# A two-layer attention and expert kernel: layer 0's sum over the experts in seven half-block products instead of eight, with two PSUM banks each for the scores and the scans

## The chip, the cores and the metric

The kernel runs on one core of a Trainium2 chip. The core has a matrix engine (TensorE, PE in the profile, with its weight loads as PEld), a vector engine (VectorE, DVE), an activation engine (ScalarE, ACT), a general engine (GpSimd, POOL) and an engine that issues DMAs (SyncE, SP). They work on an on-chip memory, SBUF, of 128 partitions; matrix products land in PSUM, which this kernel divides into 8 banks of 512 fp32 per partition. The metric is device time in microseconds. Here the median of three runs before the change is 1165.7 us (1164.95 to 1167.74). A line such as L765 is line 765 of the kernel before.

## What is computed

Tokens x (4096 x 256, fp32) go through two layers. In layer 0 every token is normalised, and two terms are added to it: a gated attention within chunks of 32 tokens, and 16 experts which all see every token, each weighted by its own sigmoid. In layer 1 there are four gated linear scans (of which the router mixes two per token) and eight larger experts, of which each token takes one. Only layer 0's experts matter to the change:

```python
def _L0_ffn_ref(input_tensor, expert_sel, keys, values):   # xn, (16, 256), (16, 256, 128), (16, 128, 256)
    sel = jax.nn.sigmoid(jnp.einsum('bsd,ed->bse', input_tensor, expert_sel))
    scores = jax.nn.relu(jnp.einsum('bsd,edh->bseh', input_tensor, keys))
    out = jnp.einsum('bseh,ehv,bse->bsv', scores, values, sel)
    return out
...
xn = _layernorm(x, axis=-1)
x = x + _L0_attn_ref(xn, ...) + _L0_ffn_ref(xn, ...)
xn = _layernorm(x, axis=-1)
x = x + _L1_attn_ref(xn, ...) + _L1_ffn_ref(xn, ...)
```

`out` is a product over the 16 x 128 pairs of expert and hidden unit: a (tokens x 2048) matrix times a (2048 x 256) matrix.

## The kernel before

**Blocks and groups.** Tokens are worked in 8 blocks of 512 (`TB`; `HB` is half, 256). Features lie on the partitions, in two halves of 128 (`DC`). The 16 experts are worked in 4 groups of 4 (`EG`), each as two pairs (`SG`).

**Seven products.** A 2 x 2 blocked matrix product can be done with 7 block products and some sums of blocks in place of 8. `seven` does that (Winograd's form): `weight_sums` prepares the sums of the weights once, `column_sums` those of the tokens per block, on GpSimd. The seven products are accumulated in three PSUM banks, `px`, `py` and `pv`; ScalarE copies `px` out between products (`u1`, `u2`, `u4`: L238, L245, L249) and VectorE adds these copies to `py` or `pv` (L239, L250, L255). The kernel uses it for the queries and gates (`yg`), for the score of each expert group (`scores`) and for layer 1's scans (`scans`). `seven` is a generator that is advanced one step at a time, so that a caller can put other work between its steps.

**The sum over the experts** is not done that way before the change: `into` (L765) takes, for each expert and each 128 tokens, the 128 x 128 scores as weights and the 128 x 256 values as the moving operand: 4 products of 256 columns per expert, 64 per block, accumulated in two PSUM banks (`acc`) together with the attention's output product. At the block's end VectorE adds the two banks to the residual (L802).

**Order.** PE, SP, ACT and DVE follow the order in which the Python code emits instructions (`manual_schedule`); each engine takes its queue in order and waits at an instruction until what it needs is there. On POOL a scheduler chose the order, other than at the start and in the tail. In `experts0` a loop over the 16 experts advances `scores` of the next group by a step, emits one expert's products, and runs what the dictionary `beside` holds for this expert: `scan_step`s of the block before, pieces of the next block's layer norm (`norm0`), pieces of the routing of the block before (`norm1`), loads. A `scan_step` advances the scans by one of four steps of `seven` and emits on VectorE up to two pieces that are due (a scan is one piece, its weighing by the router another). There are 24 scan steps per block from block 2 on, 12 in block 1 and none in block 0. At a block's start comes `attention0`, which advances `norm1` of the block before (`aside`).

**PSUM.** 8 banks: `px`, `py`, `pv` for the scans (`psc1`), `a`, `b`, `c` for scores and transposes (`ps`), two for `acc` and the attention's outputs (`pacc`). The scans swap `px` and `py` from one pair to the next (`bank_of`).

**DMA.** SP loads the next group's `keys`, `vals` and `selb` (the sigmoids, broadcast to all partitions), the scans' weights `ws`, the next x. A load waits in SP's queue until the buffer is free, and with it everything behind it.

Of the kernel before, what the change touches and what calls it, by code (L numbers as in the profile page):

```python
# [51 lines left out]
def tile_two_layers(  # L52
# [39 lines left out]
    def load_x(b, parts=1):  # L92
        xs[b] = res.tile([P, NT, D], F32, name=f"x_{b}", tag="x", bufs=5)
        rows = x[b * TB : (b + 1) * TB, :].rearrange("(n p) d -> p n d", p=P)
        for n in range(0, NT, NT // parts):
            nc.sync.dma_start(out=xs[b][:, n : n + NT // parts, :], in_=rows[:, n : n + NT // parts, :])
# [43 lines left out]
    def inverse_root(y, var):  # L140

        v = small.tile([P, NT], F32, name="v_eps")
        nc.vector.tensor_scalar(v, var, EPS, None, ALU.add)
        bits = small.tile([P, NT], I32, name="bits")
        nc.vector.tensor_scalar(bits, v.bitcast(I32), 1, None, ALU.logical_shift_right)
        nc.vector.tensor_scalar(y.bitcast(I32), bits, -1.0, float(0x5F3759DF), ALU.mult, ALU.add)
        s = small.tile([P, NT], F32, name="newton")
        for _ in range(3):
            nc.vector.scalar_tensor_tensor(s, y, -0.5, y, ALU.mult, ALU.mult)
            nc.vector.tensor_mul(s, s, v)  # L150
            nc.vector.scalar_tensor_tensor(y, s, 1.5, y, ALU.add, ALU.mult)

    def layernorm(xt, xn, mv, rstd):
# [7 lines left out]
        inverse_root(rstd, mv[:, :, 1])  # L161
        yield
        for n in range(NT):
            nc.vector.tensor_scalar(
                xn[:, n, :D], xt[:, n, :], mv[:, n, 0:1], rstd[:, n : n + 1], ALU.subtract, ALU.mult
            )

    def transposed(ps, banks, dst, src):

        for c in range(DC):  # L170
            pt = ps.tile([P, TB], F32, name="pt", tag=next(banks))
            for n in range(NT):
                nc.tensor.transpose(pt[:, n * P : (n + 1) * P], src[:, n, c * P : (c + 1) * P], ident)
            nc.scalar.copy(dst[:, c, :], pt)
            yield
# [47 lines left out]
    def seven(name, w, cols, z, bank, keep):  # L223
# [18 lines left out]
        pv = bank(f"pv_{name}")  # L242
        product(7, pv, True)
# [3 lines left out]
        product(5, px, False)  # L247
# [62 lines left out]
    banks = cycle(("px", "py", "pv"))  # L310

    def bank_of(i, name):

        return name if i % 2 or name == "pv" else {"px": "py", "py": "px"}[name]

    def plain(i, z, b, s):
        w = scan_w[i]
        for ec in range(DC):
            for q, (k, m) in enumerate(PAIRS[s]):
                p = psc1.tile([P, TB], F32, name=f"p_{i}_{ec}_{q}", tag=next(banks))  # L320
# [9 lines left out]
    def scans(b):  # L330
# [44 lines left out]
        for s in range(len(PAIRS)):  # L375
# [18 lines left out]
            else:  # L394
                it = seven(
                    f"s{i}", scan_w[i], cols1[b], z,
                    lambda n, i=i: psc1.tile([P, SG, HB], F32, name=n, tag=bank_of(i, n[:2])),
                    lambda n: su.tile([P, SG, HB], F32, name=n, tag="u", bufs=4),
# [29 lines left out]
    def room(name):  # L428

        return psc1.tile([P, 2, D], F32, name=name, tag=bank_of(steps_done // CHUNKS, "py"))  # L430
# [22 lines left out]


    HALF = (1, 2, 2, 1, 1, 2, 2, 1)
    SCANS_AT = [(0,) * E0, (0,) * len(HALF) + HALF] + [HALF + HALF] * (NB - 2)
# [3 lines left out]
    def scan_step(k=1):  # L460
        nonlocal steps_done
        for _ in range(k):
            if finished and steps_done % CHUNKS == 2 and next(finished[0], 0) == 0:
                finished.pop(0)
# [5 lines left out]
            for piece in due:  # L470
                piece()

# [12 lines left out]
    with ExitStack() as l0:  # L485
# [3 lines left out]
        pacc = l0.enter_context(tc.tile_pool(name="pacc", bufs=2, space=bass.MemoryType.PSUM))  # L489


        third = cycle(("b", "c", "a"))
        spare = repeat("c")
# [26 lines left out]
        keys, vals, ksum_d = {}, {}, []  # L520
# [20 lines left out]
        def values(i):  # L541
            g = i % (E0 // EG)
            if i in vals or i >= NB * (E0 // EG):
                return
            vals[i] = wp.tile([P, EG, D], F32, name=f"vals_{i}", tag="vals", bufs=2)
            nc.sync.dma_start(out=vals[i], in_=e_vals[:, g * EG : (g + 1) * EG])
# [20 lines left out]
        def fold():  # L567
            raw = []
            for j, w in enumerate((wq, wkk)):
                r = wk.tile([P, DC, D], F32, name=f"raw_{j}", tag="rs", bufs=3)  # L570
                pt = ps.tile([P, DC, D], F32, name=f"ptw_{j}", tag=next(third))
# [8 lines left out]
            pw = ps.tile([P, DC, D], F32, name="pw", tag=next(third))  # L580
# [27 lines left out]
        def chosen(b, xnT, bank):  # L608

            psel = ps.tile([P, P], F32, name=f"psel_{b}", tag=bank)  # L610
# [6 lines left out]
        def norm0(b, out):  # L617
# [6 lines left out]
            if b == 0:  # L624
# [3 lines left out]
                pt = [ps.tile([P, TB], F32, name=f"pt_{c}", tag=next(third)) for c in range(DC)]  # L628
# [7 lines left out]
            else:  # L636
                yield from transposed(ps, spare, xnT, xn)
# [7 lines left out]
        def sevens(name, w, cols, z):  # L645
# [3 lines left out]
                lambda n: ps.tile([P, SG, HB], F32, name=n, tag={"px": "a", "py": "c", "pv": "b"}[n[:2]]),  # L649
                lambda n: wk.tile([P, SG, HB], F32, name=n, tag=n[:2]),  # L650
            )

        def attention0(b, xnT, cols, aside):
# [6 lines left out]
            def values(n):  # L660

                if n % 2 == 0:
                    pv.append(psc1.tile([P, 2, D], F32, name=f"pv_{b}_{n}", tag=("py", "pv")[n // 2]))
# [10 lines left out]
            next(aside, None)  # L674
# [3 lines left out]
            next(aside, None)  # L678
# [13 lines left out]
            pst = ps.tile([P, NT, CHUNK], F32, name=f"pst_{b}", tag="b")  # L692
            for n in range(NT):
                for c in range(DC):
                    for q in range(0, P, CHUNK):
# [4 lines left out]
                        )  # L700
            sT = wk.tile([P, NT, P], F32, name=f"sT_{b}", tag="u1")
# [28 lines left out]
        NB_G = E0 // EG  # L730

        def experts0(b, cols, selb0, att, beside):

            rs = {}

            def scores(g):
# [10 lines left out]
                it = sevens(f"{b}_{g}", keys.pop(NB_G * b + g), cols, r)  # L747
# [15 lines left out]
            def into(n, lhsT, rhs, first, stop):  # L763

                nc.tensor.matmul(  # L765
                    acc[n // 2][:, n % 2, :], lhsT, rhs, start=first and n % 2 == 0, stop=stop, skip_group_check=True
                )

            def gated(n):
                for c in range(DC):  # L770
                    into(n, og[:, c, n * P : (n + 1) * P], wo[:, c, :], c == 0, False)

            ahead = scores(0)
            next(ahead)
            next(att)
            next(ahead)
            next(att)
            next(ahead)
            og = next(att)
            acc = [pacc.tile([P, 2, D], F32, name=f"acc_{b}_{h}", tag="acc") for h in range(NT // 2)]  # L780
            next(ahead)
            for n in range(NT):
                gated(n)
            k = 0
            for g in range(E0 // EG):
                ahead = scores(g + 1) if g + 1 < E0 // EG else iter(())
                r = rs.pop(g)
                values(NB_G * b + g + 1)
                val = vals.pop(NB_G * b + g)
                for i in range(2):  # L790
                    for q in range(SG):
                        next(ahead, None)
                        for n in range(NT):
                            into(
                                n, r[i][:, q, n * P : (n + 1) * P], val[:, SG * q + i, :], False, k == E0 - 1
                            )
                        for step in beside.get(k, ()):
                            step()
                        k += 1
            for h in range(NT // 2):  # L800
                at = xs[b][:, 2 * h : 2 * h + 2, :]
                nc.vector.tensor_add(at, at, acc[h])  # L802

        def norm1(b):
# [7 lines left out]
            side = spare if b + 1 < NB else third  # L812
            yield from transposed(ps, side, xn1T[b], xn)
            if b * len(PAIRS) < FIRST_PLAIN:
                cols1[b] = column_sums(su, xn1T[b], f"sums1_{b}", 2)
            pg = ps.tile([P, P], F32, name=f"pg_{b}", tag=next(side))
# [7 lines left out]
            pl = ps.tile([P, NT, QC], F32, name=f"pl_{b}", tag=next(side))  # L824
# [28 lines left out]
            pct = ps.tile([P, P + 2 * NT * E1], F32, name=f"pct_{b}", tag=next(side))  # L853
# [44 lines left out]
        for b in range(NB):  # L898
# [7 lines left out]
            beside = {e: [] for e in range(E0)}  # L906
            if b + 2 < NB:
                beside[8].append(lambda b=b: load_x(b + 2))
            for e, k in enumerate(SCANS_AT[b]):
                if k:  # L910
                    beside[e].append(lambda k=k: scan_step(k))
            if b > 0:
                for e in (0, 1, 2, 3, 4, 5, 6):
                    beside[e].append(lambda: next(back))
            if b + 1 < NB:
                ahead = norm0(b + 1, xnT)

                for e in (5, 7, 8, 9, 10, 12, 13) if b else (3, 4, 5, 8, 9, 12, 13):
                    beside[e].append(lambda: next(ahead))
            if b == 0:  # L920
                kept = scan_sums()
                for e in (1, 2, 3, 4, 5, 6, 7, 8, 14):
                    beside[e].append(lambda: next(kept))
            if b == 1:
                beside[0].append(lambda: scan_weights(0))
            if 1 < b < NB - 1:

                for s in ((3, 4), (5,), (0,), (1,), (2,))[b - 2]:
                    beside[5].append(lambda s=s: raw_weights(s))
# [6 lines left out]
        l0_ps, between = ps, repeat("a")  # L936

        def room(name):
            return l0_ps.tile([P, 2, D], F32, name=name, tag=next(between))

        third = cycle("bc")
        back = norm1(NB - 1)
        for _ in range(3):
            next(back)
        scan_step(4)
        next(back)
        next(back)
        next(back)
        scan_step(2)
        next(back)  # L950
        scan_step(1)
        next(back)
        scan_step(1)
        next(back)
        scan_step(4)
# [12 lines left out]
    ps = ctx.enter_context(tc.tile_pool(name="ps1", bufs=5, space=bass.MemoryType.PSUM))  # L968

# [187 lines left out]
    def first_sums7(j):  # L1157
# [40 lines left out]
        pv = psc1.tile([P, FP, P], F32, name=f"pv1_{j}", tag="pv")  # L1198
# [174 lines left out]
```

## Time and profile before

| | before |
|---|---|
| median of 3 runs | 1165.7 us (1164.95 to 1167.74) |
| the profiled execution | 1166.05 us |
| its span, first to last instruction | 1164.3 us |
| mean granted TensorE clock | 0.998 |
| start to block 0's first product | 14.8 us |
| block 0, block 1, block 2 | 69.7, 93.3, 108.9 us |
| blocks 3 to 6 | 109.4 us each |
| HBM read, written | 209.0 MB, 27.1 MB |

The blocks are taken from the start of each block's first `px_yg` product. Matmuls are pipelined: a row's mean duration (380 ns for 256 columns) overlaps that of the next one, so that the pace is read from the starts of consecutive runs, not from the durations. Every fp32 product is two records in the trace: the 512 products of L765 are 1024 records. "Idle before" is the time that the engine stood still just before the instruction, with what ended it.

### The profile page before, as it was taken

How to read it: one execution, taken by the hardware profiler on the slowest of the kernel's cores; microseconds unless marked ns; L12 is line 12 of the kernel's file. 1: busy time of each engine (PE TensorE's matmuls, PEld its weight loads, DVE VectorE, ACT ScalarE, POOL GpSimd, SP SyncE). 2: the span in 40 equal slices, each digit the busy share in tenths (PEclk: the TensorE clock that was granted, in tenths of full speed). 3: DMA queues.
4: the chain of work that ended last, by engine and by line, in shares of the span. 5: the costliest groups of instructions: out<-in, count | busy, mean ns of one | idle time of the engine just before them, and what ended most of it. 6: DMA issues, size and time to landing. Idle time of an engine off the chain costs nothing. (4 is left out here: it accounts for less than half of the span.)

```text
span 1164.3 us, 17738 instructions
## 1 busy us (share of the span) xinstructions
PE 1147.5 (99%) x6426; PEld 976.8 (84%) x6426; DVE 750.1 (64%) x1568; ACT 368.1 (32%) x719; POOL 356.5 (31%) x410
## 2 busy tenths in 40 slices
PE   8999999999999999999999999999999999999997
PEld 7887888888888888888888888888744889999996
DVE  5545736687579657866786787578699435654222
ACT  3112142344343433333342343343434211111221
POOL 6182220232014120402130222011054167774433
PEclk9999999999999999999999999999999999999999
DMA  7796464475256434634654565244247866688796
GB/s 246 233 340 242 149 216 140 156 240 186 101 185 205 155 122 171 215 136 160 213 189 136 183 204 185 102 168 155 73 148 231 304 227 216 226 296 314 264 353 240
DMA packets 90442, 233.60 MB, mean 201 GB/s; under 512 B 14076, under 2 KB 43024, under 8 KB 83440
## 3 DMA queue, kind: packets, MB, share of 16 engines
q1 hardware_dynamic: 82128, 205.00, 51.8%
q0 software_dynamic: 7792, 26.91, 6.4%
q8 instruction: 52, 0.85, 0.3%
q10 hardware_dynamic: 432, 0.52, 0.1%
q14 instruction: 38, 0.31, 0.1%
HBM read 208.98 MB, written 27.09 MB: 203 GB/s over the span
## 5 line engine op out<-in xcount | busy, mean ns | idle before, releaser
L765 PE MATMUL acc<-vals,rs 128*128 128x256 f32 x1024 | 242.2, 380 | 0.0
L765 PEld LDWEIGHTS acc<-vals,rs 128*128 128x128 f32 x1024 | 194.4, 190 | 27.0 <-issue 1.4
L1223 PE MATMUL py<-w2p,hT 128*128 128x256 f32 x576 | 133.9, 380 | 0.0
L348 POOL COPY last<-z 128x1 f32<-128x1 f32 x56 | 19.6, 352 | 340.2 <-DVE z L346 340.2
L1223 PEld LDWEIGHTS py<-w2p,hT 128*128 128x128 f32 x576 | 106.1, 191 | 12.3
L306 ACT ACTIVATE z<-z,bs 128x256 f32<-128x256 f32 (+1 forms) x156 | 87.4, 611 | 1.9 <-DVE z L255 1.9
L229 PE MATMUL px_s<-sums,ws 128*128 128x256 f32 x312 | 81.4, 383 | 0.0
L229 PE MATMUL px_s<-xn1T,ws 128*128 128x256 f32 x312 | 80.2, 380 | 0.0
L229 PE MATMUL pv_s<-sums,ws 128*128 128x256 f32 x312 | 80.1, 379 | 0.0
L1129 PE MATMUL ph<-xTp,w1p 128*128 128x128 f32 (+1 forms) x512 | 75.0, 302 | 1.5 <-ACT xTp L1113 1.5
L346 DVE TENSOR_TENSOR_SCAN z<-z,last,z 128x512 f32<-128x512 f32 x56 | 75.7, 1351 | 0.0
L1129 PEld LDWEIGHTS ph<-xTp,w1p 128*128 128x128 f32 x512 | 68.8, 192 | 5.6 <-ACT xTp L1113 2.0
L743 DVE SCALAR_TENSOR_TENSOR rs<-rs,selb 128x512 f32<-128x512 f32 x64 | 69.3, 1082 | 2.1 <-DMA selb<-sel_d 1.1
L229 PE MATMUL px<-xnT,keys 128*128 128x256 f32 x256 | 69.4, 394 | 0.1
L229 PE MATMUL px<-sums,keys 128*128 128x256 f32 x256 | 66.6, 383 | 0.0
L229 PE MATMUL pv<-sums,keys 128*128 128x256 f32 x256 | 66.6, 383 | 0.0
L229 PEld LDWEIGHTS px_s<-xn1T,ws 128*128 128x128 f32 x312 | 59.3, 190 | 8.2 <-issue 0.4
L229 PEld LDWEIGHTS pv_s<-sums,ws 128*128 128x128 f32 x312 | 59.4, 190 | 8.0
L229 PEld LDWEIGHTS px_s<-sums,ws 128*128 128x128 f32 x312 | 57.3, 190 | 9.8 <-ACT u_s L245 3.2
L322 PE MATMUL p<-xn1T,wr 128*128 128x512 f32 x144 | 63.4, 595 | 1.1 <-ACT z L325 1.1
L306 ACT ACTIVATE z<-px_s,bs 128x256 f32<-128x256 f32 x78 | 32.7, 470 | 99.1 <-PE px_s L229 99.1
L1133 ACT ACTIVATE hT<-ph,b1p 128x128 f32<-128x128 f32 (+1 forms) x68 | 27.1, 398 | 112.4 <-PE ph L1129 66.8
(264 smaller groups left out, 2017.6 us busy)
## 6 DMA issues: line engine op xcount, KB each, us to landing
ws<-wsum_d SPq DMA_DIRECT2D x39, 896.0 KB, 4.9
selb<-sel_d SPq DMA_DIRECT2D x64, 512.0 KB, 6.5
w1p<-in_w_dram SPq DMA_DIRECT2D x27, 1024.0 KB, 7.1
w2p<-in_w_dram SPq DMA_DIRECT2D x27, 1024.0 KB, 9.1
keys<-ksum_d SPq DMA_DIRECT2D x28, 896.0 KB, 10.5
vals<-in_e_vals_dram SPq DMA_DIRECT2D x32, 512.0 KB, 4.6
cb<-comb_d SPq DMA_DIRECT2D x32, 256.0 KB, 10.1
wsum_d<-wst POOLq DMA_DIRECT2D x6, 896.0 KB, 7.7
```

The source lines that it names most:

```text
L229: nc.tensor.matmul(to[:, q, :], w[:, q, at, :], cols[k - 1], start=start and q == 0, stop=True, skip_group_check=True,)
L306: nc.scalar.activation(z[ec][:, q, lo:hi], src[:, q, :], AF.Tanh if i == 1 else AF.Sigmoid, bias=bs[:, i, m, ec : ec + 1])
L322: nc.tensor.matmul(p, w[:, q, 2 * ec + c, :], xn1T[b][:, c, :], start=(c == 0), stop=(c == DC - 1))
L346: nc.vector.tensor_tensor_scan(h, a[ec][:, m % 2, :], h, 0.0 if b == 0 else state, ALU.mult, ALU.add)
L348: nc.gpsimd.tensor_copy(state, h[:, TB - 1 : TB])
L743: nc.vector.scalar_tensor_tensor(r[i][:, :, lo:hi], src, 0.0, selb[i][:, :, lo:hi], ALU.max, ALU.mult)
L765: nc.tensor.matmul(acc[n // 2][:, n % 2, :], lhsT, rhs, start=first and n % 2 == 0, stop=stop, skip_group_check=True)
L1129: nc.tensor.matmul(ph, w1s[:, c, f * P : (f + 1) * P], xTp(j)[:, c, : sn * P], start=(c == 0), stop=(c == DC - 1))
L1133: nc.scalar.activation(h[:, f, :], ph, AF.Relu, bias=b1s[:, f : f + 1])
L1223: nc.tensor.matmul(py, hT[j][:, f, n * P : (n + 1) * P], w2s[:, f, :], start=(f == 0), stop=(f == FC - 1))
```

## The change

**The sum over the experts in seven products.** The scores of a group are a 2 x 2 block matrix (two halves of the block's tokens, the two experts of a pair), and so are the values (two experts, two halves of 128 output columns). `unit` emits one of seven products, for one pair, as two matmuls of 128 tokens x 128 columns. Each of the seven is accumulated by itself over the whole block in its own quarter- or half-bank (`sums`, in four `acc` banks instead of two), with 2, 3 and 4 on top of the attention's output. At the block's end one ScalarE copy and four 128 x 256 VectorE additions combine them, and three 128 x 512 additions put them on the residual; one further such addition goes earlier, into the last group.

**The sums that it needs.** `score_sums` makes four sums of scores per group, each 128 x 512, on VectorE in block 0 and on GpSimd from block 1 on. Their buffer (tag "proj") is single and shared with `yg`. `value_sums` makes four 128 x 256 sums of the values on VectorE for the four groups of block 0; SP then writes the seven blocks to DRAM (`vsum_d`), from where the later blocks load them: 896 KB per group in place of 512.

**Banks.** Scores and scans have two banks each: `pv` takes the bank of `py` once VectorE's first addition has read it. Products 5 and 7 now stand together in the third step, 7 after 5 (before it at a block's first group, `close`). Transposes, the router's products and the scans' outputs share these banks at fixed places; the next x has four buffers instead of five.

**Order.** In place of the loop over experts there is a written order per group: `u` one unit, `X` a step of the next group's scores, `s` a scan step, the rest places at which pieces stand. `ALONE` is for groups without scans beside them. Layer norm and routing are cut into more pieces; one piece of `norm1` stays in the attention, after `pst`.

```diff
-        xs[b] = res.tile([P, NT, D], F32, name=f"x_{b}", tag="x", bufs=5)
+        xs[b] = res.tile([P, NT, D], F32, name=f"x_{b}", tag="x", bufs=4)
...
-        for _ in range(3):
+        for k in range(3):
+            if k:
+                yield
...
         product(6, px, False)
-        pv = bank(f"pv_{name}")
-        product(7, pv, True)
         u2 = keep(f"u2_{name}")
         nc.scalar.copy(u2, px)
         yield
-        product(5, px, False)
+        pv = bank(f"pv_{name}")
+        for k in (7, 5) if close else (5, 7):
+            product(k, px if k == 5 else pv, k == 7)
...
-        pacc = l0.enter_context(tc.tile_pool(name="pacc", bufs=2, space=bass.MemoryType.PSUM))
+        pacc = l0.enter_context(tc.tile_pool(name="pacc", bufs=4, space=bass.MemoryType.PSUM))
...
-            vals[i] = wp.tile([P, EG, D], F32, name=f"vals_{i}", tag="vals", bufs=2)
-            nc.sync.dma_start(out=vals[i], in_=e_vals[:, g * EG : (g + 1) * EG])
+            vals[i] = v = wp.tile([P, SG, SEVEN, P], F32, name=f"vals_{i}", tag="vals", bufs=2)
+            if i < NB_G:
+                group = e_vals[:, g * EG : (g + 1) * EG].rearrange("p (q i) (k d) -> p q i k d", i=2, k=2)
+                for at, (k, h) in ((0, (0, 0)), (5, (0, 1)), (1, (1, 0)), (2, (1, 1))):
+                    nc.sync.dma_start(out=v[:, :, at, :], in_=group[:, :, k, h])
+                vsum_d.append(dram.tile([P, SG, SEVEN, P], F32, name=f"vsum_d_{g}"))
+            else:
+                nc.sync.dma_start(out=v, in_=vsum_d[g])
+
+        def value_sums(i):
+            b11, b21, b22, t1, t2, t3, t4 = (vals[i][:, :, k, :] for k in range(SEVEN))
+            nc.vector.tensor_sub(t1, t3, b11)
...
-                lambda n: ps.tile([P, SG, HB], F32, name=n, tag={"px": "a", "py": "c", "pv": "b"}[n[:2]]),
+                lambda n: ps.tile([P, SG, HB], F32, name=n, tag={"px": "a", "py": "b", "pv": "b"}[n[:2]]),
...
+        ORDER = [
+            "y0 u s y1 u s p0 y2 u y3 u X x1 u s b0 u X x2 u s b1 u u X x3 u s u s p1 u u X x4 u".split(),
+            "u s q0 u u X x1 u s b0 u X x2 u s b1 u s p0 u u X x3 u s u u X x4 u s u".split(),
+        ]
+        ALONE = [
+            "y0 u y1 u y2 u y3 u X x1 u b0 u X x2 u b1 u u X x3 p1 u u X x4 u u u".split(),
+            "q0 u u u X x1 u b0 u X x2 u b1 u u p0 u X x3 u u X x4 u u u".split(),
+        ]
+        PARTS = (1, 2, 4, 5, 7, 6, 3)
...
+            def score_sums(g):
+                a11, a12, a21, a22 = (r[:, :, h * HB : (h + 1) * HB] for h in range(2) for r in rs[g])
+                t = wk.tile([P, 4, SG, HB], F32, name=f"rsum_{b}_{g}", tag="proj")
+                eng = nc.gpsimd if b else nc.vector
+                eng.tensor_add(t[:, 0], a21, a22)
+                eng.tensor_sub(t[:, 1], a11, a21)
+                eng.tensor_sub(t[:, 2], t[:, 0], a11)
+                eng.tensor_sub(t[:, 3], a12, t[:, 2])
...
+            def unit(g, k, q, part, val):
+                for h in range(2):
+                    nc.tensor.matmul(
+                        sums[k][:, h], part[k][:, q, h * P : (h + 1) * P], val[:, q, VAL[k], :],
...
-                    for q in range(SG):
                         next(ahead, None)
-                        for n in range(NT):
-                            into(
-                                n, r[i][:, q, n * P : (n + 1) * P], val[:, SG * q + i, :], False, k == E0 - 1
-                            )
...
-            for h in range(NT // 2):
-                at = xs[b][:, 2 * h : 2 * h + 2, :]
-                nc.vector.tensor_add(at, at, acc[h])
+                if b == 0:
+                    nc.sync.dma_start(out=vsum_d[g], in_=val)
+            c1, c2 = (wk.tile([P, 2, D], F32, name=f"c_{b}_{k}", tag=k) for k in ("u2", "u4"))
+            both16 = wk.tile([P, 2, P], F32, name=f"both16_{b}", tag="u1")
+            nc.scalar.copy(c1[:, :, :P], sums[1])
+            nc.vector.tensor_add(both16, sums[6], c1[:, :, :P])
+            nc.vector.tensor_add(c1[:, :, P:], sums[5], both16)
+            nc.vector.tensor_add(c2[:, :, :P], sums[7], both16)
+            nc.vector.tensor_add(c2[:, :, P:], sums[5], c2[:, :, :P])
+            nc.vector.tensor_add(xb[:, :2, :], xb[:, :2, :], acc[0])
+            nc.vector.tensor_add(xb[:, :2, :], xb[:, :2, :], c1)
+            nc.vector.tensor_add(xb[:, 2:, :], xb[:, 2:, :], c2)
...
-        for _ in range(3):
+        for _ in range(7):
             next(back)
-        scan_step(4)
+        scan_step(5)
```

## The prediction

> **What bounds the kernel now.** I read the busy times first, then the costliest groups, then the starts of consecutive runs on PE (to get a pace, since durations overlap), and last the table of stretches and VectorE's and GpSimd's order of time.
>
> ```profile
> PE 1147.5 (99%) x6426; PEld 976.8 (84%) x6426; DVE 750.1 (64%) x1568; ACT 368.1 (32%) x719; POOL 356.5 (31%) x410
> L765 PE MATMUL acc<-vals,rs 128*128 128x256 f32 x1024 | 242.2, 380 | 0.0
> ```
>
> PE is the bound: 99% of 1164.3 us. A product taken away from it is worth its pace, as long as nothing new makes PE wait. The pace is in PE's order of time (start, duration, line):
>
> ```profile
> 502.12 1.89 PE L765 MATMUL acc<-vals,rs 128*128 128x256 f32 x8
> 503.85 0.38 PE L229 MATMUL px_s<-xn1T,ws 128*128 128x256 f32 x1
> ...
> 1091.62 3.73 PE L1129 MATMUL ph<-xTp,w1p 128*128 128x128 f32 x32
> 1095.19 0.38 PE L1111 MATMUL px<-ident,xrp 128*128 128x128 f32 x2
> ```
>
> Eight records of 256 columns take 503.85 - 502.12 = 1.73 us, 0.216 each. Thirty-two of 128 columns take 1095.19 - 1091.62 = 3.57 us, 0.1115 each. Half the columns cost almost exactly half the time, so half-sized products lose only 0.1115 - 0.108 = 0.0035 us per record.
>
> The stretches of block 0 (first row, no scans beside it) and of block 4 (second) show what VectorE has left; columns are busy us of PE, PEld, DVE, ACT, POOL, granted clock, DMA share, GB/s:
>
> ```profile
> 33.50:84.00 50.50, 50.50 (x252) 44.19 (x251) 23.25 (x47) 6.71 (x12) 25.19 (x33) 1.00 0.86 284
> 505.50:615.00 109.50, 109.50 (x613) 94.47 (x612) 81.21 (x169) 41.58 (x83) 21.79 (x26) 1.00 0.51 172
> ```
>
> VectorE is busy 74% of a block, GpSimd 20%, and the clock is full.
>
> **The change part by part.**
>
> *Products.* Before: 1024 x 0.216 = 221.2 us. After: 8 blocks x 4 groups x 7 units x 2 pairs x 2 matmuls x 2 records = 1792 records, x 0.1115 = 199.8. That is **-21.4 us**. The pace would have to reach 221.2 / 1792 = 0.123 to give it all back. Bounds: -21.4 at the pace of L1129; at the 190 ns that one weight load of L765 lasts, were loads not hidden, it would be a loss of 119, but L1129 has the same loads and runs at 0.1115, so I leave that end out.
>
> *Block 0's sums on VectorE.* Each group gets four value sums (128x256) and four score sums (128x512). Nearest rows:
>
> ```profile
> L1163 DVE TENSOR_TENSOR tsum<-xTp 128x128 f32<-128x128 f32 x8 | 2.3, 281 | 0.0
> L356 DVE TENSOR_TENSOR acc<-acc,z 128x512 f32<-128x512 f32 x48 | 38.2, 796 | 1.6
> ```
>
> 281 ns for 128 columns and 690 to 796 for 512 put 256 columns near 0.42 to 0.53; with 0.7 to 0.9 for the score sums a group costs 4.9 to 6.9 us, four groups 20 to 28. VectorE has 50.5 - 23.2 = 27 us free there, so it comes close to being full, and the scores of the next group queue behind the sums. Laying this out group by group I find PE waiting between 1 and 5.2 us for the whole block; the middle is **+3**. The six extra DMA issues on SP (0.43 to 0.6 us each, 3 us) delay `selb`: 20.48 + 7.1 = 27.6 becomes 30.6, and the first use is at 32.4, so nothing. The writes of `vsum_d` wait in SP's queue for the value sums of their own group, long done when SP, which has issued the next group's loads ahead of them, comes to them: nothing; uncovered, each would hold the loads behind it by one issue (0.6).
>
> *GpSimd's score sums, blocks 1 to 7.* 28 groups x 4 sums, of 1.27 (L1152) to 1.53 us (L341) each: 142 to 171 us on an engine that is 20% busy. Time on GpSimd is free; what it does to VectorE is not. Four rows bear on this:
>
> ```profile
> L1152 POOL TENSOR_TENSOR wsum<-w1p 128x512 f32<-128x512 f32 x8 | 10.3, 1286 | 0.1
> L1164 DVE TENSOR_TENSOR tsum<-xTp,tsum 128x128 f32<-128x128 f32 x8 | 10.1, 1262 | 0.3
> ```
> ```profile
> 598.68 1.21 DVE L355 TENSOR_TENSOR z<-z,cb 128x512 f32<-128x512 f32 x1
> 599.93 1.10 DVE L356 TENSOR_TENSOR acc<-acc,z 128x512 f32<-128x512 f32 x1
> ```
>
> L1164 runs while GpSimd is in its sums of L1152 to L1155 and takes 1262 ns; L1163, the same size, takes 281: one VectorE addition lost 0.98 us, about a whole GpSimd sum, and the four additions L1163 to L1166 together no more than 1.0. Between 596.3 and 600.4, with four smaller GpSimd sums running, L355 and L356 lose 0.5 each over their usual 0.7: 1.1 per set. So four sets add 4.0 to 4.4 us of VectorE to a block. The trace has no case with GpSimd sums in every group; bounds are nothing and L1164's full wait behind each of the four, 4 x 0.98 = 3.9 us per set. I take 1.1, since both places where it can be seen gave that.
>
> The Trainium skill, "SBUF — State Buffer", section "Who interferes with whom", speaks against this part: VectorE instructions with two operands in SBUF and GpSimd instructions that read SBUF exclude each other, the later one blocked for the other's whole length. The 1262 ns agree with it, the 1.1 us of a whole set do not reach its worst case: an estimate from that rule, with four sums of 1.29 us each blocking an addition, is 5.1 us per set, and with it the whole change would come out as a loss of some 50 us.
>
> What reaches PE is less, as VectorE runs beside PE. PE needs it in time at two kinds of place: product 7, which now overwrites the bank that L239 must have read, and the transposes, which need `xn`. Between the `py` product and product 7 of the same bank stand at least 5.2 us; L239 follows its product by 0.83 us in the median, 3.1 at most: 2.1 us of cover against a set's 1.1. Laying a steady block out by hand, PE waits 0.8 us without contention (0.5 and 0.3 at transposes in groups 0 and 2) and 3.3 with 1.1 us added in each set (1.5, 0.5, 1.3). Block 4 already has some 2.6 us of small gaps per 100 us, which these partly replace, so I take 1.5 per block, for the six blocks with full scans (2 to 7): **+9**. Bounds: 0, and 4 x (3.9 - 2.1) x 6 = 43.
>
> *The block's end.* VectorE does four 128x256 and three 128x512 additions, 4 x 0.43 + 3 x 0.7 = 3.8 us, against 1.28 in L802's pair, ahead of `yg`'s L239. `yg` issues 6.05 us of products before product 7 needs L239 done, and it is done at about 5.65: covered by 0.4 us; uncovered up to 2.5 per block. At layer 0's end the longer chain stands ahead of the last norm, with five scan steps to cover it, not four: **+0.5** (0 to 2.5).
>
> *Two banks, loads, GpSimd's order.* The swap of `pv` into `py`'s bank is priced in the cover above. `vals` grows by 0.39 MB in 28 groups, 11 MB, plus 3.7 MB written, at a DMA share of 0.51: nothing; were they not hidden, 384 KB more at block 4's 172 GB/s are 2.3 us per group. The x load goes from two blocks ahead to one, in the first group; the first layer norm on it stands in the second group, over 25 us later, and a load lands in under 11 (the longest of the page's rows): nothing. GpSimd's own queue is passed too: the router's four scatter issues (L884, 1.18 us each) stand ahead of the third group's score sums, and end about when the sums' buffer comes free; uncovered, all 4.7 us come late, against a first use some 9 us after the group begins: nothing. The column sums (0.73, 0.87, 1.40 us) stand ahead of the fourth group's score sums; those give their first result about 7 us after the group begins, and the fourth product needs it at 9: nothing, or a group's start late by up to 1.
>
> Sum: -21.4 + 3 + 9 + 0.5 = -8.9. From the profiled execution's 1166.05 that is 1157.15; the median of the runs is 0.35 below that execution, so **1157**.
>
> **The rivals.** With x for the third term, the change is x - 17.9. A measurement of this kernel can tell about 0.3%, 3.5 us, from no change.
>
> *Waits stay small* (18%): gaps only replace those there are, x = 0 and block 0 at +1: -20, 1146 (1143 to 1150). For it: 2.1 us of cover. Against: the hand layout finds transposes late.
>
> *The gain is given back* (18%): x between 14.4 and 21.4, or 2.4 to 3.6 us per block, near the 3.3 of the layout: 1167 (1162 to 1169).
>
> *Slower* (20%): in each group, VectorE's additions after L239 alternate with GpSimd's four sums, each waiting for one. A set then costs up to 3.9, L239 gets later than its cover, product 7 waits in the shared bank, and the scores behind it are late for the next sums. At 6 us per block x is 36: 1184. It decides from 3.6 us per block on. For it: L1164 shows the full wait; 81.2 + 2.6 + 4 x 3.9 = 99.4 us of VectorE in a block of 106.7 (109.4 less a block's 2.7). Against: no set in this trace lost more than 1.1.
>
> *The forecast* (44%): 1157, own range 1150 to 1162.
>
> **How the numbers follow.** Faster is forecast and small waits, 0.62; same 0.18; slower 0.20. The range takes in the forecast, the given-back case, most of small waits and the lower edge of slower: 1144 to 1173.
>
> **What would show it.** Starts of eight unit records 0.89 us apart confirm the first term. Steady blocks of some 108.2 us (109.4 - 2.7 + 1.5), with L356 and L743 longer in the mean and GpSimd busy near 500 us, confirm the third; blocks near 106.7 mean small waits, 110.3 and more the slower case, with PE's idle time named after the scores' L239 or GpSimd's sums. Block 0 should stay near 69.7 (- 2.7 + 3). I am wrong in kind if unit records keep 0.12 or more, or if PE waits for a load.

## The result, and the profile after

The changed kernel takes 1223.13 us in the median (1222.99 to 1228.84), the kernel before 1165.86 on the same chip: 1.0501 times as long, 95% interval 1.0468 to 1.0534. The forecast was 1157. The profiled execution has a span of 1221.2 us, 56.9 more than before:

| stretch | before | after | difference |
|---|---|---|---|
| start to block 0 | 14.8 | 14.2 | -0.6 |
| block 0 | 69.7 | 82.35 | +12.7 |
| block 1 | 93.3 | 98.3 | +5.0 |
| blocks 2 to 6, each | 108.9 to 109.4 | 115.4 to 116.5 | +33.5 in all |
| block 7's first px_yg to the end | 439.8 | 446.2 | +6.4 |

Busy time by engine, from the page of the changed kernel:

```profile
PE 1153.2 (94%) x7194; PEld 992.1 (81%) x7194; DVE 850.1 (70%) x1648; ACT 376.9 (31%) x727; POOL 499.0 (41%) x522
```

PE is busy 94% of a longer span; it now stands still in every block. PE's order of time shows that the cheaper products are real (start, duration, line):

```profile
82.09 1.50 PE L828 MATMUL acc<-vals,rsum 128*128 128x128 f32 x12
83.43 2.02 PE L828 MATMUL acc<-vals,rs 128*128 128x128 f32 x16
```

Twelve unit records take 1.34 us, 0.1117 each: 1792 of them 200.2 us, 21.0 less than before. The waits of PE, longest in total first (total us, times, longest):

```profile
PE pt L179 <- DVE rs L246: 25.2, 13, 4.9
PE pct L925 <- DVE z L246: 6.2, 5, 1.2
PE acc L828 <- DVE vals L559: 4.3, 1, 4.3
```

L246 is VectorE's first addition after a `py` product (L239 before). The transposes of the layer norm (`pt`) and the router's products (`pct`) use the bank that it must have read. So PE waits for a bank of the shared pair, and not for GpSimd's sums: no line names them. The place is the same in each steady block; here it is in block 4, VectorE's order of time first, then PE's and GpSimd's:

```profile
500.67 1.58 DVE L357 TENSOR_TENSOR z<-z,cb 128x512 f32<-128x512 f32 x1
502.29 1.65 DVE L358 TENSOR_TENSOR acc<-acc,z 128x512 f32<-128x512 f32 x1
...
504.46 1.70 DVE L348 TENSOR_TENSOR_SCAN z<-z,last,z 128x512 f32<-128x512 f32 x1
506.08 1.16 DVE L151 SCALAR_TENSOR_TENSOR newton<-rstd 128x4 f32<-128x4 f32 x1
...
507.55 0.68 DVE L357 TENSOR_TENSOR z<-z,cb 128x512 f32<-128x512 f32 x1
508.26 0.69 DVE L358 TENSOR_TENSOR acc<-acc,z 128x512 f32<-128x512 f32 x1
508.88 0.68 DVE L343 TENSOR_TENSOR z<-z 128x512 f32<-128x512 f32 x1
509.48 0.73 DVE L169 TENSOR_SCALAR xn<-x,mv,rstd 128x256 f32<-128x256 f32 x2
510.12 0.68 DVE L246 TENSOR_TENSOR rs<-py,u 128x512 f32<-128x512 f32 x1
```
```profile
505.81 0.59 PE L236 MATMUL py<-xnT,keys 128*128 128x256 f32 x2
...
507.55 1.03 PE L236 MATMUL pv_s<-sums,ws 128*128 128x256 f32 x4
510.86 0.44 PE L179 MATMUL pt<-ident,xn 128*128 128x128 f32 x2 [2.28 <-DVE rs L246]
```
```profile
500.44 1.26 POOL L797 TENSOR_TENSOR rsum<-rs,rs 128x512 f32<-128x512 f32 x1 [0.42 <-PE acc L828]
501.67 1.72 POOL L798 TENSOR_TENSOR rsum<-rs 128x512 f32<-128x512 f32 x1
503.35 1.72 POOL L799 TENSOR_TENSOR rsum<-rsum,rs 128x512 f32<-128x512 f32 x1
505.15 2.07 POOL L800 TENSOR_TENSOR rsum<-rs,rsum 128x512 f32<-128x512 f32 x1
```

The `py` product ends near 506.2 and the transposes in its bank are due at 508.4. L246 gets its turn at 510.1, behind everything that VectorE was late with. While GpSimd is in its four sums, a Newton step on 128x4 elements takes 1.16 us (0.16 elsewhere) and the scan 1.70 (1.27 elsewhere); earlier in the same set L357 and L358 took 1.58 and 1.65 for 0.68. L246 itself, which reads one operand from PSUM, keeps its 0.68. That set cost VectorE 0.9 + 1.0 + 0.4 + 1.0 = 3.3 us. The groups of the changed kernel say the same over the whole span:

```profile
L358 DVE TENSOR_TENSOR acc<-acc,z 128x512 f32<-128x512 f32 x48 | 47.7, 994 | 1.6
L151 DVE SCALAR_TENSOR_TENSOR newton<-rstd 128x4 f32<-128x4 f32 x48 | 21.9, 457 | 0.8
```

Before, the two had means of 796 (L356) and 185 ns (L149). The Trainium skill ("SBUF — State Buffer", "Who interferes with whom") has a VectorE instruction with two operands in SBUF and a GpSimd instruction that reads SBUF shut each other out; the 1.16 us of a 0.16 us instruction beside a sum of 2.07 fit that.

### The profile page after: what moved, and what is told of

It is laid out like the page before. It is cut to its first block, busy times and chain, and to the rows that moved or that the text cites. A ratio compares the mean times of both kernels' runs of the same rounds, so it can differ in the third digit from the quotient of the medians.

```text
span 1221.2 us, 19575 instructions
## 1 busy us (share of the span) xinstructions
PE 1153.2 (94%) x7194; PEld 992.1 (81%) x7194; DVE 850.1 (70%) x1648; ACT 376.9 (31%) x727; POOL 499.0 (41%) x522
## 5 line engine op out<-in xcount | busy, mean ns | idle before, releaser
L828 PEld LDWEIGHTS acc<-vals,rsum 128*128 128x128 f32 x1024 | 139.5, 195 | 8.4 <-issue 1.4
L828 PE MATMUL acc<-vals,rsum 128*128 128x128 f32 x1024 | 143.8, 279 | 0.0
L828 PE MATMUL acc<-vals,rs 128*128 128x128 f32 x768 | 112.2, 282 | 5.0 <-DVE vals L559 4.3
L828 PEld LDWEIGHTS acc<-vals,rs 128*128 128x128 f32 x768 | 106.4, 198 | 11.7 <-DVE vals L559 5.1
L797 POOL TENSOR_TENSOR rsum<-rs,rs 128x512 f32<-128x512 f32 x28 | 35.5, 1268 | 172.7 <-PE acc L815 141.3
L348 DVE TENSOR_TENSOR_SCAN z<-z,last,z 128x512 f32<-128x512 f32 x56 | 82.3, 1470 | 0.0
L236 PE MATMUL px<-sums,keys 128*128 128x256 f32 x256 | 72.9, 410 | 0.0
L236 PEld LDWEIGHTS pv_s<-sums,ws 128*128 128x128 f32 x312 | 58.9, 190 | 12.5 <-DVE x L447 4.7
L955 POOL DMA_INDIRECT xs_d<-xn,pos_i x32 | 32.9, 1028 | 85.8 <-DVE run L953 78.5
L236 PE MATMUL px<-xnT,keys 128*128 128x256 f32 x256 | 66.7, 383 | 0.0
```

The costliest lines, as they stand in the source:

```text
L236: nc.tensor.matmul(to[:, q, :], w[:, q, at, :], cols[k - 1], start=start and q == 0, stop=True, skip_group_check=True,)
L348: nc.vector.tensor_tensor_scan(h, a[ec][:, m % 2, :], h, 0.0 if b == 0 else state, ALU.mult, ALU.add)
L797: eng.tensor_add(t[:, 0], a21, a22)
L828: nc.tensor.matmul(sums[k][:, h], part[k][:, q, h * P : (h + 1) * P], val[:, q, VAL[k], :], start=(k in (1, 5) and g == 0 and q == 0 and h ...
L955: to = nc.gpsimd.indirect_dma_start(out=xs_d, out_offset=bass.IndirectOffsetOnAxis(ap=pos_i[:, n : n + 1], axis=0), in_=xn[:, n, :], in_of ...
```

## The experiments

Six of the kernels leave work out, so that tokens go to other experts in layer 1; they are read by their blocks. From layer 1's first expert product to the last, e1 and e3 take 262 us where the kernels with the whole computation take 255. The kernel before took 1168.2 us beside e1 to e4, 1165.0 beside e5 to e8, 1165.1 beside e9 to c1 and 1165.2 beside c2.

**e1, no sums of scores.**
```diff
-                eng.tensor_add(t[:, 0], a21, a22)      # and the other three sums
...
-                return {... 5: t[:, 0], 7: t[:, 1], 6: t[:, 2], 3: t[:, 3]}
+                return {... 5: raw, 7: raw, 6: raw, 3: raw}      # raw = xnT[b][:, :, :HB]
```


> Left out: score_sums; the units of products 5, 7, 6 and 3 read xnT, which is always ready, in place of the four sums. Nothing else is changed: banks, order and the sums of the values stay. Theory (contention: GpSimd's four sums per group lengthen VectorE's additions, VectorE comes late to the additions that free a PSUM bank and to xn, PE waits at the transposes): steady blocks fall from 116.4 to about 108 us, block 1 from 98 to 93, block 0 from 82 to 74; about 1160 us in all. Rival 1 (two banks and the new order make PE wait with or without the sums): steady blocks stay above 113 us, 1200 us or more in all. Rival 2 (PE waits for the sums themselves, as GpSimd delivers them late): as the theory here, 1160; the next kernel parts them.

Steady blocks 108.1, block 1 88.7, block 0 81.2; 1176.8 us. The sums cost a steady block 8.0 us (blocks 3 to 6: 7.3 to 8.4). Banks and order don't (rival 1 falls). Block 0 doesn't follow the theory.

**e2, the sums on VectorE in all blocks.**
```diff
-                eng = nc.gpsimd if b else nc.vector
+                eng = nc.vector
```


> score_sums on VectorE in all blocks, not only in block 0. Theory: VectorE itself takes 4 x 0.68 = 2.7 us per group for them, 11 us per block, against the 8 us that a steady block lost to contention; so PE's waits stay of the same size, steady blocks 113 to 118 us, 1205 to 1235 in all, but VectorE's other instructions go back to their usual durations. Rival 1 (banks and order): within 5 us of 1223. Rival 2 (GpSimd delivers late): the sums come 3 us after the group begins, not 7, and steady blocks fall below 110 us, 1185 or less in all.

Steady blocks 115.5 to 117.1, 1221.9 us, as the theory had it (the total fits rival 1 as well, which e1 has ruled out). L357 is back at 721 ns and L151 at 166 in the mean, and yet nothing is gained: four sums in a row on VectorE are worth as much as GpSimd's interference.

**e3, no sums at all.** As e1, and in block 0:
```diff
-                if b == 0:
-                    value_sums(g)
```


> Left out: score_sums as in the run before, and value_sums: in block 0 SP loads raw blocks of the values in all seven places (three DMA issues more per group). Theory: block 0 falls to 68 us (69.7 less 2.7 for the products, and a little for the longer block end), as the sums' VectorE time beside GpSimd's sums of weights was what made it 82; about 1152 in all. Rival 1: block 0 stays above 75 and the total above 1195.

Steady blocks 108.1 again, but block 0 takes 86.4, more than with the sums: VectorE's sums alone are not what makes it long. Total 1181.5. The steady block has this share of each engine (columns as before), and the changed kernel's block 5 that:

```profile
512.83:620.93 108.10, 107.40 (x708) 94.93 (x707) 82.45 (x176) 42.51 (x83) 18.62 (x26) 1.00 0.53 188
```
```profile
542.22:658.71 116.49, 109.92 (x709) 95.82 (x708) 90.71 (x176) 42.87 (x83) 41.35 (x42) 0.99 0.50 174
```

With equally many VectorE instructions (176), GpSimd's sums add 8.3 us to VectorE's busy time (90.71 - 82.45), 2.1 us per set, and the block is 8.4 us longer.

**e4, eight products in the new order.** The 16 old products of a group (expert and 128 tokens) are spread over the 14 `u`; two banks each, no sums, the short block end.
```diff
-                        k, q = next(units)
-                        unit(g, k, q, part, val)
+                        for i, q, n in next(slots):
+                            nc.tensor.matmul(acc[n // 2][:, n % 2, :], r[i][:, q, n * P : (n + 1) * P], val[:, SG * q + i, :], ...)
```


> The sum over the experts as before the change, 8 products of 256 columns, 64 per block, spread over the 14 places u of the new order; no sums, no longer block end; two banks each and the new order stay. Theory: 1166 us, within 8, blocks 69 to 71 and 109 to 111. Rival 1 (banks and order): steady blocks 115 or more, 1200 us or more.

1170.9 us, block 0 70.8, steady blocks 110.4: the banks and the order cost 1.0 us per steady block. Against e3's 108.1 the units save 2.3 per block where they stand, the longer block end included.

**e5, no writes of the values' sums.**
```diff
-                if b == 0:
-                    nc.sync.dma_start(out=vsum_d[g], in_=val)
-                nc.sync.dma_start(out=v, in_=vsum_d[g])
+                nc.sync.dma_start(out=v, in_=ksum_d[g])
```


> Left out: the four writes of the values' sums to DRAM in block 0 (3.7 MB); the later blocks load as many bytes from the keys' sums, so that only block 0 has less to move. All sums are made as in the changed kernel. To be read by block, as the tokens' routing differs. Theory now (block 0 is bound by its DMA queues, whose share is 0.9 there, not by VectorE's sums: without any sums it took 81 and 86 us): block 0 falls from 82.3 to 73 us or less. Rival (VectorE's sums beside GpSimd's make block 0 long): block 0 stays above 79. Steady blocks 116 in both.

Block 0 stays at 82.8 (1234.1 us in all): the writes alone aren't it either.

**e6, the sums made but not used.**
```diff
+                return {... 5: raw, 7: raw, 6: raw, 3: t[:, 3]}
```


> GpSimd makes the four sums of scores as in the changed kernel, but only product 3, the group's last, reads them; products 5, 7 and 6 read xnT. To be read by block. If the sums cost through VectorE's time (contention), steady blocks stay at 115 to 117 us; if PE lost its time by waiting for sums that GpSimd delivers late, they fall to the 108 of the run without sums.

Steady blocks 115.8 to 118.0 (1234.3 in all), and the same first wait of PE as in the changed kernel:

```profile
PE pt L179 <- DVE rs L246: 25.1, 13, 4.9
```

Three of the four sums are read by no product, and the time is lost all the same. So it is lost through VectorE, not through sums that come late.

**e7, the sums on VectorE, spread.**
```diff
                         k, q = next(units)
+                        if (k, q) in ((2, 0), (4, 0), (5, 0), (7, 0)):
+                            next(made)()      # the next of the four sums, on VectorE
```


> The four sums of scores on VectorE in all blocks, as in the run e2, but each emitted by itself, four units ahead of its first use, not all four at the group's start. If the place in VectorE's queue is what makes L246 and xn late (a stretch of 2.7 us ahead of them), steady blocks fall from e2's 115 to 117 to 108 to 111 us and the whole to 1170 to 1185. If VectorE's total time is the limit (95 us of 116), they stay above 114 and the whole above 1205.

Steady blocks 110.0 to 111.9, 1188.0 us: the first alternative, with two of five blocks and the total just above its ranges. VectorE works as long as in the changed kernel, but PE waits little:

```profile
297.07:407.82 110.75, 108.18 (x708) 94.63 (x707) 91.69 (x192) 42.66 (x83) 21.32 (x26) 1.00 0.52 184
```
```profile
PE pct L926 <- DVE z L246: 8.6, 5, 1.7
```

91.7 us of VectorE in a block of 110.75 here, 90.7 in 116.49 there. VectorE's total isn't the limit; what stands in front of the instruction that frees a bank is. Of PE's 25 us of waits at the transposes 1.6 are left, and one of 1.7 per block at the router's products. Spreading the sums on GpSimd wasn't tried.

**e8, fillers on PE.**
```diff
+            for k in range(36):
+                nc.tensor.transpose(t[:, k % NT * P : (k % NT + 1) * P], ones, ident)
```


> The changed kernel with 36 transposes of a constant (some 4 us of PE) put into each of the two places in block 0 where PE stood still for 5.1 and 4.6 us. They delay nothing, as PE waits for VectorE there. Theory (the granted clock falls to half after PE has stood still, and the 5.2 and 3.5 us stretches of half pace after the gaps come from that): both stretches are gone, the clock of block 0 is 0.98 or more in place of 0.94, block 0 is 3 to 4 us shorter, the whole 1216 to 1220. Rival (the clock falls for another reason, such as the DMA load): block 0 within 1 us of 82.3.

The clock follows as expected at the first place. The changed kernel, then e8 (columns as in the stretches above; the clock is the third figure from the right):

```profile
74.00:76.00 2.00, 2.00 (x8) 1.73 (x8) 0.00 (x0) 0.59 (x1) 1.62 (x3) 0.50 0.91 163
```
```profile
74.00:76.00 2.00, 2.00 (x18) 1.92 (x17) 0.00 (x0) 0.99 (x2) 1.76 (x4) 1.00 1.07 354
```

The half pace from 71.5 to 76.7 is gone. The second stretch stayed, behind a gap of 2.0 us that was left. But block 0 is 81.7, not 3 to 4 us shorter, and the whole 1228.8. By its time block 0 fits the rival (within 1 us of 82.3); it is the clock's figures that speak for the theory. The time size was wrong, as PE came to the next wait earlier and waited longer there.

**e9, neither sums nor writes** (e3 and e5 together).


> Left out: the sums of scores, the sums of values and the writes of the latter (the three parts that the runs e1, e3 and e5 took away one or two at a time, while block 0 stayed at 81 to 86 us). To be read by block. Theory (block 0 has two causes, each enough by itself: VectorE's sums beside GpSimd's sums of weights, and the writes, which the loads of the values two groups on wait for, with the scores' selb behind them in SP's queue): block 0 falls to 68 to 72 us. Rival (a third cause, such as the four smaller loads of the values, or the order): it stays above 76.

Block 0 takes 74.5: the theory's direction, 2.5 us above its range; 1162.2 in all, with steady blocks of 108.1. The seven smaller loads of the values per group are left, but that they are the rest wasn't tried.

**e10, e7 without the writes** (e7 and e5 together).


> Left out: the writes of the values' sums (the later blocks load the keys' sums). The score sums on VectorE, spread as in run e7; the value sums stay together at the group's start. To be read by block. Theory of two causes: block 0 at 72 to 77 us, as half of VectorE's stretch at a group's start (the value sums) is left. If the writes had nothing to do with e7's 82.0, it stays there.

Block 0 takes 78.4, just above the range, 3.6 less than e7; 1192.2 in all.

**c1, eight products in blocks 0 and 7.**
```diff
+            eight = b in (0, NB - 1)
+                if b == 1:
+                    value_sums(NB_G + g)
+                        if (k, q) in ((4, 0), (5, 0), (7, 0), (6, 0)):
+                            next(made)()
+                        if b == 1 and (k, q) == (5, 0):
+                            nc.sync.dma_start(out=vsum_d[g], in_=val)
```


> Seven products in blocks 1 to 6 only, eight in blocks 0 and 7; the values' sums are made and written in block 1, the writes half-way through a group; score sums on VectorE, each two units ahead of its first use (four in e7). Theory: block 0 as with eight products, 70.8; steady blocks 110 to 112 as in e7; from the last unit to layer 1's first expert 72 us, not 76, as the longer block end is gone from block 7; the whole 1170 to 1180, still above before. If the later place of the sums frees VectorE ahead of the router's products (pct), steady blocks fall to 108.5 to 110 and the whole to 1160 to 1168.

1198.2 us, above both expected ranges. Block 0 is 70.2 as expected; steady blocks 113.1 to 114.6 are worse than e7's, for a new reason:

```profile
PE acc L834 <- DVE rsum L804: 22.1, 16, 1.8
PE acc L834 <- DVE rsum L803: 6.6, 6, 3.0
```

Two units ahead is too late: now PE does wait for the sums.

**c2, three units ahead** (the edit is to c1).
```diff
-                        if (k, q) in ((4, 0), (5, 0), (7, 0), (6, 0)):
+                        if (k, q) in ((2, 1), (4, 1), (5, 1), (7, 1)):
```


> As c1, with each sum emitted three units ahead of its first use: c1's two left PE waiting for the sums themselves (7 us per block, no wait longer than 2), e7's four left VectorE late for the bank that the router's products use (1.9 us per block). A unit comes every 1.9 us, so nearly all of c1's waits should go without e7's coming back: steady blocks 108 to 109.5 us (109.4 before the change, 108.1 without any sums), block 1 at 92 to 95, the whole 1162 to 1172: no loss any more, and no gain that can be told from none, since the sums have to be paid and the units give 2.7 us a block at most. If spreading trades one wait for the other, steady blocks stay at 111 or more, 1178 or more in all.

1183.5 us in the median, 1.0158 times the kernel before (1.0131 to 1.0184). Steady blocks 111.1 to 112.1, block 1 96.0. The second alternative: of the waits for sums 2.6 us are left, the one for the bank is back:

```profile
PE pct L949 <- DVE z L246: 8.4, 5, 1.7
PE pt L179 <- DVE rs L246: 3.6, 10, 0.5
```

No version with the whole computation beat the kernel before. The most that the units could give in this order is seen in e3 against before: 109.4 - 108.1 = 1.3 us per steady block with the sums for nothing.

## Why the prediction was wrong

The kernel got slower where it was forecast faster. What the prediction calls block 4 (505.5 to 615) is block 5 in the count from block 0 used here. By its steps:

- **Products: right.** -21.4 forecast, -21.0 by the measured pace.
- **GpSimd's score sums: the step that failed.** +1.5 us per steady block; measured 8.0 (e3 against the changed kernel, blocks 3 to 6). Three sizes in it were wrong. The loss of a set was taken as 1.1 us, from the two places in the old trace where sets happened to meet few two-operand instructions; it is 2.1 in the mean and 3.3 in the set shown. And the cover of 2.1 us was counted up to product 7, 5.2 us behind the `py` product; but the transposes use that bank too, 2.2 us after the `py` product's end in the group shown. The layout by hand had them wait for `xn` alone. Last, "3.1 at most" for L239 holds for the scans' additions; the scores' own ended 5.9 us after its product once in each of blocks 2 to 6 of the kernel before, behind routing and layer norm, where PE didn't have to wait for it:

```profile
575.71 1.03 PE L229 MATMUL py<-xnT,keys 128*128 128x256 f32 x4
581.96 0.69 DVE L239 TENSOR_TENSOR rs<-py,u 128x512 f32<-128x512 f32 x1
```

  Block 1 was left out of the term; there the score sums cost 9.6 us (98.3 against 88.7 in e1 and e3).
- **The slower rival was the mechanism,** VectorE's two-operand instructions alternating with GpSimd's sums and a shared bank freed late, over its threshold of 3.6 us per block. It held 20%. PE waits at the transposes and the router's products, not at product 7, and the price of 6 per block was too low. The estimate from the skill's rule, a loss of some 50 us, came near the 57 measured, in part by luck: it holds 5.1 us per set where 2.1 was measured, 3 for block 0 where 15.4 was, and nothing for block 1.
- **Block 0: wrong.** +3 forecast; 12.7 + 2.7 = 15.4 measured. VectorE's added time was met, 27 us (58.9 busy, 31.7 before) of 20 to 28, though the prices given add up to 4.5 to 5.7 per group and not to 4.9 to 6.9. What stands behind these sums in VectorE's queue was not met: PE waits 4.9 us at the transposes, for an L246 behind eight of them, and 4.3 for the value sum L559. The runs showed two causes that hide each other:

| block 0 | VectorE's sums | writes | us |
|---|---|---|---|
| changed kernel | value and score sums together | yes | 82.3 |
| e5 | together | no | 82.8 |
| e7 | score sums spread | yes | 82.0 |
| e10 | score sums spread | no | 78.4 |
| e1 | value sums only | yes | 81.2 |
| e3 | none | yes | 86.4 |
| e9 | none | no | 74.5 |
| c1, e4 | none, eight products | no | 70.2, 70.8 |

  One is VectorE's sums beside GpSimd's work (the value sum L558 took 3.96 us at 85.5 in the changed kernel, beside four GpSimd additions to x, L619, and one of the tokens' sums, L223; 0.42 alone). The other was priced at nothing: the writes hold `vals`, so that the load two groups on waits for them, with `selb` behind it in SP's queue. SP's waits in that block of the changed kernel:

```profile
SPq L552 <- DMA vsum_d<-vals: 14.4, 1, 14.4
SPq L549 <- DMA vsum_d<-vals: 9.2, 2, 5.2
```

  With the sums gone, VectorE waits for `selb`: 14.0 us in all in e3's block 0, 5.1 in that of e9, which has no writes either. The line of e3:

```profile
DVE rs L772 <- DMA selb<-sel_d: 14.0, 3, 9.3
```

  Why e3 is longer there than the changed kernel stays open; it has three more loads per group. The table of stretches showed block 0's DMA share of 0.86; the step asked whether the writes have to wait, and not who waits for them.
- **The block's end:** nothing per block holds within the 1.4 us by which e3's 108.1 exceeds 106.7 (1.0 of it e4 shows without the longer end). At layer 0's end +0.5 was forecast: from the last unit to layer 1's first expert product it is 76.2 us, 71.9 before, +4.4, as the router's products wait for the later norm. With eight products in block 7 it is 73.7 (c1), with eight everywhere 71.8 (e4); what the rest in c1 is stays open.
- **Two banks, order and loads: nearly nothing,** 1.0 us per steady block (e4). The steady blocks' DMA share stayed at 0.50.

## What to carry to other kernels

An engine that is 74% busy has no free quarter: what counts is how much stands in its queue ahead of the instruction that frees a resource, and every user of that resource has to be looked up, not only the one that the change adds. Work moved to an idle engine that shares memory access with a busy one is priced by the worst rows that the trace shows, since quiet averages come from places where the two seldom met. A write out of a buffer holds the buffer: follow the next load into it, and the queue behind that load.

## What the hardware showed that was not expected

PE's granted clock fell to half around short waits of PE, during them or up to some 1.5 us after. Block 2 of the changed kernel:

```profile
277.76 0.44 PE L179 MATMUL pt<-ident,xn 128*128 128x128 f32 x2 [2.28 <-DVE rs L246]
...
279.17 1.06 PE L828 MATMUL acc<-vals,rs 128*128 128x128 f32 x4
280.03 1.91 PE L236 MATMUL px<-sums,keys 128*128 128x256 f32 x4
281.73 0.54 PE L828 MATMUL acc<-vals,rsum 128*128 128x128 f32 x3
```

After the wait, four 256-column records take 281.73 - 280.03 = 1.70 us, where they take 0.87 elsewhere; the clock is 0.50 from 278.4 to 281.8. Behind the first microseconds, the changed kernel has nine such stretches of 3.4 or 6.8 us, 41 in all, with PE busy in 35.5 of them, and a mean clock of 0.982 (0.998 before): up to 18 us, if half of that busy time reached the end, which e8 shows it doesn't. What one stretch costs is seen where blocks differ by it. In the changed kernel block 4, at full clock, takes 115.4 us, and blocks 3, 5 and 6, with one stretch of 3.4 us each, 116.3 to 116.5; in e2 it is 115.5 and 117.0, in e7 110.8 and 111.9. So about 1 of the 8.0 us that the sums cost a steady block came through the clock.

The Trainium skill ("TensorE: Matmul & The Clock Gate", "What's actually happening") gives the half clock after an idle window of some 3.4 us. Here a wait of 2.28 us was enough, and in e7 one of 1.71 (ending at 467.3); another of 2.28, ending at 510.9, was not followed by it, nor was the one of 2.50 in the trace of before (ending at 90.6). A free-running window, of which that section speaks, fits this: in each of the 14 traces all changes of the clock lie on a grid of 3.41 us. Behind the first 15 us, every step of this grid at full clock in which PE was idle for 2.0 us or more was followed by the half clock, and none with less than 1.5; between the two, both occur. The wait shown above lies in one step (275.0 to 278.4), the one at 510.9 reaches over the border of two (510.5). So a new wait of PE can cost more than its length. One of the changed kernel's four runs took 1228.8 us at a mean clock of 0.978, the others 1223 at 0.980 to 0.983.
